# A group-normalised row LSTM: the second half's scale in two parts, and the work around the first row of the loop rearranged

## The chip, the cores and the metric

The kernel runs on one core of a Trainium2 chip. The time is the device time of one execution in microseconds; with several runs it is their median. The engines are TensorE (PE; its weight loads are PEld), VectorE (DVE), ScalarE (ACT), GpSimd (POOL) and SyncE (SP, which here only issues transfers). All arithmetic is in float32.

## The reference

The input x has shape (8, 96, 128, 128): images, channels, rows, columns. It is group-normalised (32 groups of three channels, statistics over a whole image), and then a row LSTM runs down the 128 rows, each row needing the state of the row above; the result is added to x.

```python
its = conv_1x3(_gn(x), W_is * mask) + b_is      # input taps: left and own column
def step(carry, row_in):                        # scan over the 128 rows
    h, c = carry
    ss = conv_3(h, W_ss) + b_ss                 # state taps: left, own, right column
    gates = ss + row_in                         # 4*96 channels
    f, i, o = sigmoid(...); g = tanh(...)       # four gates in three blocks of 32 channels
    c_new = f * c + i * g
    h_new = o * tanh(c_new)
    return (h_new, c_new), h_new
out = x + hs
```

## The kernel before

**Two halves and two stages.** The eight images are two halves of four (`NH` = 2, `BH` = 4). Stage one reads all of x once for the statistics of the group norm. Stage two is a loop of 256 half steps: half step n is row n // 2 of half n % 2. Two half steps are under way at a time, so that one half's gates are made while TensorE works on the other's products.

**The statistics.** An image goes through a ring of six buffers in six chunks of 2048 columns (`CH`), each of them four pieces of 512. VectorE takes the statistics of a chunk piece by piece (`bn_stats`, L676). Chunks 2 and 4 of all images but the last are ScalarE's (`sums_of`): it needs a column `base`, the negative of the chunk's first column, as a bias, which GpSimd makes (L207). It then sums the chunk and its squares (L208, L211). `merge` on GpSimd joins both engines' figures. A ring buffer is filled again when its reader is done.

**The scale.** `Scale` makes from the statistics the scale `rstd` and the shift `nmr` of a half: `means` and `squares` are small products on TensorE with the group matrix `gm`; `to_sbuf` copies their results from PSUM to SBUF for GpSimd; `scale` adds the epsilon, makes a first guess of the inverse root with two integer operations on VectorE (L275, L280), and refines it in three rounds.

**Work placed among the statistics.** The dictionary `events` holds what is issued after a certain statistics piece: `at(image, n)` is the n-th of 24 pieces of an image. Half 0 has its scale at images 4 (`at(4, 1)` to `at(4, 6)`), its first row's taps at images 4 and 5, and its first half step at images 5 and 6 (`begin` and the entries after it). Every engine works through its own instructions in the order in which they are issued.

**The row's operands.** `hx` holds the previous row's state in 96 partitions and, in the last 32, the normalised channels 64 to 96 of the row, which share the product with the state (`normalise_shared`, `shared_rows`). Of `hx` come three moving operands: the total `vs` and the difference `vf` on VectorE and the shifted differences `vd` on GpSimd, which is told to start after VectorE's (`shifted`). The other 64 channels' taps are `xs`, made by `widen` (normalise into even and odd columns, into `xw` or, for rows 1 to 3 of the first block of half 1, into a buffer of the ring called `late`) and `combine` on GpSimd (`own_image`, `own_row`).

**The half step.** TensorE's products are named by a figure or letter and a block: 1 with `vs`, 2 with `vf`, 0 and 3 with `vd`, P, Q and E with `xs`; the blocks A, B, C are 128 gate channels each, in one PSUM bank. `cp` copies a block's first half with the bias (ScalarE, or VectorE for block A), and `lo` and `hi` on VectorE make the even and odd columns of it, which 0 and 3 then add to. `ta` and `si` are tanh and sigmoid, `fg gt ce th ou` the cell, `S F D` the next row's total, difference and shifted difference, `re` the residual. `PERIOD` is the order of one half step in the loop; a part already done is skipped, and `'`, `+` and `*` stand for the half step before, the next and the one after that.

**The hand-over.** After the last statistic, half 1's scale is made (on VectorE), then its first row's shared channels, operands and own taps, then the taps of rows 1 to 3, then the products of half step 1 in the order of `do(1, ...)`, and the loop begins. `spin` issues products that nobody reads.

## Time and profile before

| What | Figure |
|---|---|
| Median of three runs | 2081.72 us (2080.5 to 2082.07) |
| The profiled execution | 2080.96 us |
| Its span, first to last instruction | 2079.2 us |
| Mean granted TensorE clock | 0.990 |
| Last statistic of VectorE ends | 136.47 us |
| First product of half step 1 starts | 144.83 us |
| First product of half step 2 (2A) starts | 160.19 us |
| PE busy from 160.19 us to the end | 1910.94 of 1919.01 us |

Times within the profile are counted from the first instruction. The device time is 1.76 us longer than the span. In the timeline a line is a group of equal instructions: start, time in us, engine, source line, operation, output and inputs, how many; in brackets the idle time before it and what ended it. In the chain of waits a line is a start, a time and what the end of the program waited for. In a table of windows each engine has its busy time and, in brackets, its instructions; behind them stand the granted clock of TensorE, the share of the transfer engines and GB/s.

### The profile page before, as it was taken

To read this page: it belongs to the slowest core of one execution; us is meant where nothing else is said; L and a number is where in the kernel's file an instruction comes from. 1 tells how busy PE (TensorE), PEld (TensorE's weight loads), DVE (VectorE), ACT (ScalarE), POOL (GpSimd) and SP (SyncE) were. 2 spreads that over 40 slices of the span, in tenths; PEclk is the share of its full clock that TensorE was granted. 3 is DMA by queue.
4 is the path that set the end of the run, shared out by engine and by line. 5 is a ranking of instruction groups with operands and counts; after the bars stand their busy time and mean duration, and the time that the engine had idled before them with its cause. 6 is when DMAs were issued, how large, how long until landed. Compare 5 with 4: busy or idle time off the path is not lost.

```text
span 2079.2 us, 31230 instructions
## 1 busy us (share of the span) xinstructions
PE 1950.6 (94%) x10810; PEld 1588.2 (76%) x10810; DVE 1684.7 (81%) x3494; ACT 1355.3 (65%) x2389; POOL 1435.0 (69%) x1615
## 2 busy tenths in 40 slices
PE   0249999999999999999999999999999999999998
PEld 0138888888888888888888888888888888888886
DVE  5677888888888888888888888888888888888887
ACT  4656666666666666666666666666666666666666
POOL 2326877777777777777777777777777777777762
PEclk9969999999999999999999999999999999999999
DMA  9991434443333444333334443333444333344411
GB/s 380 403 321 35 112 92 112 112 112 88 76 81 91 112 112 112 96 74 89 89 102 112 112 107 78 80 92 92 112 112 112 91 76 80 90 112 112 112 31 31
DMA packets 103325, 236.24 MB, mean 114 GB/s; under 512 B 5953, under 2 KB 8897, under 8 KB 97281
## 3 DMA queue, kind: packets, MB, share of 16 engines
q1 hardware_dynamic: 103168, 234.25, 41.2%
q8 instruction: 87, 1.43, 0.3%
q14 instruction: 70, 0.57, 0.1%
HBM read 183.90 MB, written 50.33 MB: 113 GB/s over the span
## 4 chain that ended last, share of the span: by engine, by line
PE 93%; DMA 3%; ACT 2%; POOL 1%; DVE 1%; issue 0%; SPq 0%; ACTq 0%; POOLq 0%; DVEq 0%
PE ps L384 92%; DMA piece<-in_x_dram 1%; DMA wt<-in_w_own_dram 1%; DMA xs<-in_x_dram 1%; ACT piece L208 0%; ACT piece L211 0%; ACT xs L208 0%; ACT xs L211 0%; DVE bst L676 0%; PE pv L246 0%; ACT g L436 0%; POOL xs L322 0%; POOL xs L321 0%; POOL xw L304 0%; ACT piece L302 0%
## 5 line engine op out<-in xcount | busy, mean ns | idle before, releaser
L384 PE MATMUL ps<-vd,wl 128*128 128x256 f32 x3072 | 815.7, 388 | 3.7 <-DVE ps L433 3.7
L436 ACT ACTIVATE g<-ps 32x512 f32<-32x512 f32 x768 | 453.6, 591 | 455.2 <-PE ps L384 446.8
L384 PEld LDWEIGHTS ps<-vd,wl 128*128 128x128 f32 x3072 | 562.5, 190 | 155.9 <-issue 86.5
L484 POOL TENSOR_TENSOR vd<-hx 128x512 f32<-128x512 f32 x256 | 265.9, 1039 | 483.9 <-DVE vs L474 480.5
L384 PE MATMUL ps<-xs,wx 64*128 64x256 f32 x3072 | 459.1, 395 | 14.9 <-POOL xs L321 14.9
L384 PE MATMUL ps<-vs,wm 128*128 128x256 f32 x1536 | 458.4, 380 | 0.0
L384 PE MATMUL ps<-vf,wm 128*128 128x256 f32 x1536 | 457.6, 380 | 0.0
L440 ACT ACTIVATE ps<-ps 96x512 f32<-96x512 f32 x768 | 418.6, 572 | 16.5 <-PE ps L384 0.2
L384 PEld LDWEIGHTS ps<-xs,wx 64*128 64x128 f32 x3072 | 323.6, 187 | 123.7 <-issue 84.9
L444 DVE TENSOR_TENSOR ps<-ps,c 96x512 f32<-96x512 f32 x256 | 178.0, 695 | 266.7 <-ACT ps L440 266.7
L433 DVE TENSOR_TENSOR ps<-m,ps 128x256 f32<-128x256 f32 x768 | 329.3, 429 | 26.3
L429 DVE TENSOR_TENSOR ps<-m,ps 128x256 f32<-128x256 f32 x768 | 324.9, 423 | 13.8 <-ACT m L426 5.0
L501 POOL TENSOR_TENSOR x<-x,hx 96x512 f32<-96x512 f32 x254 | 328.7, 1294 | 0.0
L384 PEld LDWEIGHTS ps<-vs,wm 128*128 128x128 f32 x1536 | 292.4, 191 | 40.6 <-DVE vf L479 0.7
L384 PEld LDWEIGHTS ps<-vf,wm 128*128 128x128 f32 x1536 | 292.5, 190 | 40.5 <-DVE vf L479 0.4
L426 ACT ACTIVATE m<-ps,wl 128x256 f32<-128x256 f32 x513 | 243.0, 474 | 74.0 <-PE ps L384 60.3
L322 POOL TENSOR_TENSOR xs<-xw 128x512 f32<-128x512 f32 x253 | 270.1, 1068 | 0.0
L384 PE MATMUL ps<-xs,wt 64*128 64x256 f32 x1536 | 265.3, 377 | 0.1
L454 ACT ACTIVATE th<-c 96x512 f32<-96x512 f32 x256 | 161.5, 631 | 105.5 <-DVE c L450 105.5
L304 POOL TENSOR_SCALAR hx<-x,rstd,nmr 32x512 f32<-32x512 f32 x248 | 199.9, 806 | 25.5
L384 PEld LDWEIGHTS ps<-xs,wt 64*128 64x128 f32 x1536 | 195.6, 188 | 18.6 <-issue 0.7
L304 POOL TENSOR_SCALAR xw<-xr,rstd,nmr 128x512 f32<-128x512 f32 x252 | 203.6, 808 | 0.8 <-DMA xr<-in_x_dram 0.4
(94 smaller groups left out, 1265.3 us busy)
## 6 DMA issues: line engine op xcount, KB each, us to landing
xr<-in_x_dram SPq DMA_DIRECT2D x124, 512.0 KB, 6.7
x<-in_x_dram SPq DMA_DIRECT2D x63, 768.0 KB, 5.8
out_dram<-x SPq DMA_DIRECT2D x62, 768.0 KB, 4.7
xs<-in_x_dram SPq DMA_DIRECT2D x30, 1024.0 KB, 11.9
piece<-in_x_dram SPq DMA_DIRECT2D x16, 1024.0 KB, 10.8
x<-in_x_dram SPq DMA_DIRECT2D x62, 256.0 KB, 3.1
xs<-in_x_dram SPq DMA_DIRECT2D x4, 512.0 KB, 7.8
out_dram<-x SPq DMA_DIRECT2D x2, 576.0 KB, 3.7
```

The costliest lines, as they stand in the source:

```text
L304: engine.tensor_scalar(dst, src, scale, shift, ALU.mult, ALU.add)
L322: nc.gpsimd.tensor_sub(differences, strided(xw[:, 0, :], 0, [(W + 1, n), (J, 2), (1, J)]), strided(xw[:, 0, :], J + 1, [(W + 1, n), (0, 2) ...
L384: nc.tensor.matmul(self.ps[a][:, bass.ts(half, HB)], weights[rows, bass.ts(a, P)], rhs[rows], start=new, stop=False, skip_group_check=True,)
L426: nc.scalar.activation(self.m1[a], m1, AF.Identity, bias=column)
L429: nc.vector.tensor_add(self.ps[a][:, 0:HB], self.m1[a], self.ps[a][:, HB:])
L433: nc.vector.tensor_sub(hi, self.m1[a], hi)
L436: nc.scalar.activation(self.g[a * 32 : (a + 1) * 32], self.ps[a][C:P], AF.Tanh)
L440: nc.scalar.activation(gate, gate, AF.Sigmoid)
L444: nc.vector.tensor_mul(f, f, self.c)
L454: nc.scalar.activation(self.th, self.c, AF.Tanh)
L484: diff = nc.gpsimd.tensor_sub(self.vd.rearrange("p t (b j) -> p t b j", b=BH), strided(h, 1, [(BH * JP - 1, 2), (JP, BH), (1, J)]), stride ...
L501: (nc.gpsimd if row + 1 < NT else nc.vector).tensor_add(xo, xo, self.h)
```

## The change

- The column `base` is made by ScalarE itself, with an activation of scale -1.
- `Scale` takes a range of images. Half 1 has two of them: the first three images' scale is made during the last image's statistics (`next_means`, `squares`, `to_sbuf`, `variance`, `guess`, at `at(7, 1)` to `at(7, 13)`), with GpSimd refining it, and only the last image's after them (`final`).
- `next_row`, at `at(7, 13)`, makes the first row of these three images: shared channels and widening on ScalarE; total, difference, shifted difference and own taps on GpSimd. What is left of the row after the last image is that image's.
- Half 0's variance moves from `at(4, 6)` to `at(4, 5)`, and its guess and scale to `at(4, 13)`.
- The memset of the buffer for rows 1 to 3 comes before the last image's scale. These rows' shared channels go from ScalarE, behind the own taps, to GpSimd, ahead of them.
- `do(1, ...)` has the own taps directly after blocks A and B's first products; 1C, 2C, the copies and the even and odd columns are left to `PERIOD`'s first round.

```diff
     def sums_of(b, i, xc):
         if i == 0:
-            nc.gpsimd.tensor_scalar(base[:, b : b + 1], xc[:, 0:1], -1.0, None, ALU.mult)
+            nc.scalar.activation(base[:, b : b + 1], xc[:, 0:1], AF.Identity, scale=-1.0)
...
     class Scale:
-        def __init__(self, s):
-            self.st, self.rstd, self.nmr = st[s], rstd[s], nmr[s]
+        def __init__(self, s, lo, hi):
+            n, self.name = hi - lo, f"{s}_{lo}"
+            self.st, self.rstd, self.nmr = (
+                st[s][:, lo:hi], rstd[s][:, :, lo:hi], nmr[s][:, :, lo:hi]
+            )
...
+        def variance(self, engine):
+            engine.tensor_scalar(self.v, self.pv, GN_EPS, None, ALU.add)
+
+        def guess(self):
...
+            nc.vector.tensor_scalar(
+                bits, self.v.bitcast(integer), 1, None, ALU.arith_shift_right
+            )
+            nc.vector.tensor_scalar(
+                self.rstd.bitcast(integer), bits, 0x5F3759DF, -1.0, ALU.subtract, ALU.mult
+            )
...
-        def total(self):
-            e, o = self.pair()
-            self.vs = self.tile("vs", (P, HB))
-            self.last = nc.vector.tensor_add(self.vs.rearrange("p (b j) -> p b j", b=BH), e, o)
+        def total(self, engine=nc.vector, lo=0, hi=BH):
+            e, o = self.pair(lo, hi)
+            self.last = engine.tensor_add(self.operand("vs")[:, 0, lo:hi], e, o)
...
+    def next_means():
+        merge(1, BH - 1)
+        late.append(Scale(1, 0, BH - 1))
+        late[0].means()
+
+    def next_row():
+        late[0].scale(nc.gpsimd)
+        shared_rows(nc.scalar, 1, 0, 1, range(BH - 1))
+        for j in range(BH - 1):
+            widen(nc.scalar, xw[1], j, 1, 1, j, 0)
+        step = half_step(1)
+        step.total(nc.gpsimd, 0, BH - 1)
+        step.difference(nc.gpsimd, 0, BH - 1)
+        step.shifted(0, BH - 1)
+        own_row(xw[1], 1, 0, 0, BH - 1)
...
-        at(4, 6): lambda: A.scale(nc.gpsimd),
+        at(4, 5): lambda: A.variance(nc.gpsimd),
+        at(4, 13): lambda: (A.guess(), A.scale(nc.gpsimd)),
...
-        at(7, 1): lambda: merge(1, BH - 1),
+        at(7, 1): next_means,
+        at(7, 4): lambda: (late[0].squares(nc.scalar), late[0].to_sbuf()),
+        at(7, 6): lambda: late[0].variance(nc.gpsimd),
+        at(7, 13): lambda: (late[0].guess(), next_row()),
...
-    Bh = Scale(1)
-    Bh.means()
-    Bh.squares(nc.vector)
+    rows = ring[2][:, 0 : (R - 1) * BH * (W + 1)].rearrange("p (r q) -> p r q", q=W + 1)
+    nc.gpsimd.memset(rows[:, :, J : J + 1], 0.0)
+    final = Scale(1, BH - 1, BH)
+    final.means()
+    final.squares(nc.vector)
     spin(5, wt[0][:, 0:256])
-    Bh.scale(nc.vector)
-
-    shared_rows(nc.vector, 1, 0, 1)
-    do(1 - NH, "S F")
+    final.variance(nc.vector)
+    final.guess()
+    final.scale(nc.vector)
+    shared_rows(nc.vector, 1, 0, 1, (BH - 1,))
+    step = half_step(1)
+    step.total(lo=BH - 1)
+    step.difference(lo=BH - 1)
+    widen(nc.scalar, xw[1], BH - 1, 1, 1, BH - 1, 0)
+    own_row(xw[1], 1, 0, BH - 1, BH)
+    step.shifted(BH - 1, BH)
+
     for j in range(BH):
-        widen(nc.scalar, xw[1], j, 1, 1, j, 0)
-    own_row(xw[1], 1, 0)
-    do(1 - NH, "D")
-    late = ring[2][:, 0 : (R - 1) * BH * (W + 1)].rearrange("p (r q) -> p r q", q=W + 1)
-    nc.gpsimd.memset(late[:, :, J : J + 1], 0.0)
-    for j in range(BH):
-        widen(nc.scalar, late, j, R - 1, 1, j, 1, step=BH)
+        widen(nc.scalar, rows, j, R - 1, 1, j, 1, step=BH)
+    shared_rows(nc.gpsimd, 1, 1, R)
     for r in range(1, R):
-        own_row(late[:, (r - 1) * BH : r * BH], 1, r)
-    shared_rows(nc.scalar, 1, 1, R)
+        own_row(rows[:, (r - 1) * BH : r * BH], 1, r)
...
-    do(1, "1A 2A 1B 2B 1C 2C PA PB QA QB P+A PC QC cpA loA hiA cpB loB hiB cpC loC hiC")
+    do(1, "2A 1A 2B 1B PA PB QA QB PC P+A QC")
```

## The prediction

> **What bounds the kernel now.** I read the page first (busy shares, then the shares of the chain), then the chain of waits in the gap between the two stages, then the timelines of single engines there, and last the one-microsecond windows with the granted clock. From the page:

> ```profile
> PE 1950.6 (94%) x10810; PEld 1588.2 (76%) x10810; DVE 1684.7 (81%) x3494; ACT 1355.3 (65%) x2389; POOL 1435.0 (69%) x1615
> PE 93%; DMA 3%; ACT 2%; POOL 1%; DVE 1%; issue 0%; SPq 0%; ACTq 0%; POOLq 0%; DVEq 0%
> ```

> TensorE (PE) carries the row loop. In the windows from 160.19 us to the end, PE is busy 1910.94 of 1919.01 us, and the change leaves the loop's order from the second half step on as it is. So it can only move what lies before 160.19: the statistics (VectorE's last one ends at 136.47) and the hand-over to the loop. The chain of waits in the hand-over:

> ```profile
> 146.14 1.03 POOL vd L484
> ...
> 147.28 0.74 ACT piece L302
> ...
> 150.33 0.74 ACT hx L302
> ...
> 153.35 0.48 ACT m L426
> ...
> 153.86 0.44 DVE ps L429
> ...
> 154.32 0.44 DVE ps L433
> ...
> 154.81 10.29 PE ps L384 x42
> ```

> GpSimd's shifted difference holds up the memset queued behind it (147.12); that holds ScalarE's four late widenings (`piece`, 3.03 us), then four shared rows (`hx`, 3.00 us), and only then comes the copy of block B (`m`), on which VectorE's even/odd pair and TensorE's product 0B wait. TensorE sees it so:

> ```profile
> 140.42 4.61 PE L171 MATMUL spin<-wl 128*128 128x256 f32 x10
> 144.83 1.06 PE L384 MATMUL ps<-vs,wm 128*128 128x256 f32 x2
> ...
> 148.06 2.00 PE L384 MATMUL ps<-xs,wx 64*128 64x256 f32 x14
> 150.78 1.10 PE L384 MATMUL ps<-vd,wl 128*128 128x256 f32 x4 [0.72 <-DVE ps L433]
> 154.81 1.22 PE L384 MATMUL ps<-vd,wl 128*128 128x256 f32 x2 [2.93 <-DVE ps L433]
> ...
> 160.19 0.59 PE L384 MATMUL ps<-vf,wm 128*128 128x256 f32 x2
> ```

> One product is two records. Two stalls, 0.72 and 2.93 us; at 160.19 the next half step begins. The windows (PEclk is the figure behind the engines) show a second loss:

> ```profile
> 151.00:152.00 1.00, 0.88 (x4) 0.43 (x3) 0.00 (x0) 0.93 (x3) 1.00 (x2) 1.00 1.02 246
> 152.00:153.00 1.00, 0.00 (x0) 0.00 (x0) 0.00 (x0) 0.97 (x2) 1.00 (x3) 0.88 1.08 227
> 153.00:154.00 1.00, 0.00 (x0) 0.00 (x0) 0.14 (x1) 0.97 (x3) 1.00 (x2) 0.50 1.10 223
> ...
> 159.00:160.00 1.00, 1.00 (x6) 0.34 (x5) 0.00 (x0) 0.24 (x1) 0.00 (x0) 0.71 0.46 100
> ```

> The clock falls in the long stall and stays at half until 159.x.

> **The change part by part: the load stage.**
> ScalarE's own column. Seven columns leave GpSimd. On ScalarE I take 0.2 us each, from its nearest rows (128x4 Square 0.17, 128x8 copy 0.18); bounds 0.1 and 0.35. It takes away waits of 11.55 us (image 1, behind the weights) and 5.05 us (image 4, behind the half-0 scale on GpSimd). But transfers bound most of this stage: their share is 1.0 in nearly every 4 us window to 136. The one hole is 88 to 92 (0.63, some 1.5 us), after image 4's late column kept a ring slot. It should close.
> That 1.5 us should not reach the end. From 103.44 to 134.7 VectorE is busy except for one wait of 0.83 us; it, not the transfers, is then the bound, and its start follows GpSimd's four own images. So I follow VectorE.
> Half 0's variance moves one slot up and its guess from (4,6) to (4,13). Today VectorE stands 3.59 us for it (to 80.63). In the new place the first piece of chunk 3, due at 80.4 by the 2.49 us pace of the chunks, ends at 81.06; the guess follows and GpSimd's scale starts at 81.6 instead of 81.16, less the 0.19 us column: own images +0.25 us. All of `begin` follows them: +0.25. Image 6's column stands in ScalarE's queue ahead of the cell tanh (116.48): +0.2. So VectorE starts image 7 0.45 us late, and the new guess (two operations, 0.2 us each) adds 0.4. Its wait for the last transfer (0.49) absorbs the rest: +0.36 at 136.47. Bounds: 0 to +1.0.
> At (7,1) to (7,13), three images' scale. The 14 merge operations end at about 125.2 (124.8 today); half 0's chain from merge to variance took 3.4 us (77.2 to 80.6), so 128.7. VectorE reaches (7,13) at about 129.85, so it does not wait; margin 1.1 us. GpSimd's 14 scale operations take 4 us (half 0: 81.16 to 85.09), to 134.3; six ScalarE pieces of 0.42 us beside it. GpSimd's total, difference, shifted difference and own row of three images, by its rows 128x256 0.64 and 128x512 1.06: 0.54 + 0.54 + 0.85 + 0.54 + 0.85 = 3.3 us, then the memset 0.12: done near 139.5. The final image's first GpSimd work comes at 143.3, so this costs nothing; uncovered it would cost 3 to 7 us. The three images' means stand in PE's queue ahead of the spin of ten, which only shifts. SyncE issues the same transfers in the same order.

> **The hand-over.** The final image's chain (aggregate, seven small products, 15 small VectorE operations at 0.2) is as long as today's: sizes 1 and 2 instead of 4 and 8 save nothing at 0.17 us each. Scale and shift ready: 142.40 + 0.36 = 142.8.
> VectorE then does one shared row (0.35) instead of four (1.51), and total and difference of 64 columns, 0.2 each; up to 0.4 beside GpSimd's own row, as today's difference took 0.87 beside GpSimd and 0.43 without. Ready by 144.0. But TensorE is in its spin of five until about 144.7: today the last weight load of the spin ended at 144.31 and the first product loaded at 144.59, so the lead is worth little. First product at 145.05 against 144.83: +0.2.
> GpSimd: own row of one image (0.33 + 0.43), shifted difference 0.43, to 144.7; four shared rows of 32x384, by the row 32x512 at 0.80 at most 0.8 each: 147.9; three own rows at 1.68: 152.9, against 155.26 today. First reader of those is the half step after next, near 158.
> ScalarE: one widening 0.42, then four at 0.74, 142.9 to 146.3. The four shared rows are off it. The copy of B is behind nothing then.
> TensorE: 2A 1A 2B 1B, own taps from 147.4 (today 144.83 to 147.1 for the same four), seven own products 2.0 to 149.4, 1C 2C 0.86, 0A 3A 0.86, 0B at 151.1. VectorE's side: copy of A 1.16 after the own taps start, as today (148.06 to 149.22), then copy, two even/odd pairs, 0.52 + 4 x 0.46, and 0.15 to the reader: 0B may start 3.67 us after the own taps start; TensorE arrives after 3.72. A tie; I take 0.2 us of waits, bounds 0 and 0.8.
> The sum: stalls 0.72 + 2.93; the stretch 154.81 to 160.19 (5.38 us) at full clock is 0B 0.43, eight own products 1.92 (as at 172.77 to 174.69), 3B 0.54 = 2.89, so 2.49 back. 6.14 - 0.2 (start) - 0.2 (waits) = **5.7 us**.
> The profiled execution's own 2080.96 would become 2075.3, its span 2073.5. The median shown, 2081.72, is 0.76 above the profiled one; I take the gain from it: **2076.0**.

> [...] The row shows the clock falling 1 us into the stall (0.88 in 152 to 153). I go with the row: 5.7. [...]

> **The rivals.**
> 1. The clock stays low in part: the stall goes, but short waits or a later rise keep half clock for the new stretch. [...] Against: today clock 1.00 from 146 to 152 across a 0.72 us wait. Gain 2.5 to 4: 2078.5. Chance 0.15.
> 2. More: the later spin leaves TensorE warm at the final image, the spin of five takes 2.2 us less, and the product starts when the difference lands (144.1), or the closed transfer hole shows at the end. Against: after the spin today the clock was down 3.5 us later. Gain 7 to 8.7: 2073.7. Chance 0.08.
> 3. It does not do what it says: another wait takes the copy's place (late rows on GpSimd holding its next work, or the own row of the final image), or the guess eats it. GpSimd's 5 us of slack speaks against. Gain 0 to 2: 2080.7. Chance 0.05.
> 4. Slower: the second guess stands in VectorE's stream at (7,13), with eleven statistics queued behind it and the last of them the bound. If the variance comes after 129.85, each microsecond of wait is one at the end. The point from which it decides is 5.7 us: variance after 135.6. The chain would have to take twice half 0's 7.0 us (73.56 to 80.6); at 137.8 the time is 2084.0. Half 0's guess did wait 3.59 us, but one slot after its copies. Chance 0.03, half of it past 0.2%.

> **How the numbers follow.** The main case has 0.69, gain 4.3 to 7.3. About 0.2% (4.2 us) is what a measurement of this kernel can tell from no change. Faster: main 0.68, rival 2 0.08, a little of rival 1: 0.78. Slower 0.02. Same 0.20. The range runs from 2073.2 to 2079.3: down to rival 2, up over rival 1; outside lie rivals 3 and 4 and the ends of the others.

> **What would show it.** Right: no stall over 0.5 us on PE between the spin of five and the loop, clock 1.00 from about 146.5 on, ScalarE's copy of B near 149, the loop's second half step at 154.5, VectorE's last statistic within 1 us of 136.8, no hole at 88 to 92. Wrong: a wait of VectorE for GpSimd's variance at (7,13); clock at 0.5 after 148; PE waiting for `xs` from GpSimd after 155; or a row loop longer than 1919 us.

## The result, and the profile after

| | before | after |
|---|---|---|
| Median of six runs each | 2081.48 us (2080.50 to 2082.07) | 2075.69 us (2074.33 to 2077.35) |
| Ratio of after to before | | 0.9973, 95% interval 0.9961 to 0.9986 |
| Profiled execution, its span | 2080.96, 2079.15 us | 2074.40, 2072.62 us |
| Last statistic ends | 136.47 us | 137.39 us |
| First product of half step 1 | 144.83 us | 145.11 us |
| 2A of the second half step | 160.19 us | 153.68 us |
| From there to the end | 1918.96 us | 1918.95 us |

The change makes the kernel 5.8 us faster. (The 1919.01 us given for before counts to the rounded span of 2079.2.) The three stretches say where the 6.5 us between the two spans lie: last statistic +0.92, hand-over (last statistic to 2A) 23.72 to 16.29, which is -7.43, and row loop -0.01. The page of the kernel after, busy shares and shares of the chain:

```profile
PE 1950.5 (94%) x10824; PEld 1589.7 (77%) x10824; DVE 1683.4 (81%) x3493; ACT 1356.9 (65%) x2398; POOL 1441.1 (70%) x1632
PE 93%; DMA 3%; DVE 2%; ACT 1%; POOL 1%; issue 0%; SPq 0%; POOLq 0%
```

The shares hardly move: the work is the same, and a gain of 0.3% in one stretch doesn't show here. The chain of waits in the hand-over, kernel after:

```profile
137.41 0.82 DVE st L721
...
140.63 0.85 PE dm L252 x4
141.48 3.79 PE spin L171 x10
145.27 19.76 PE ps L398 x110
```

Before, the chain ran through GpSimd's `vd`, ScalarE's `piece`, `hx` and `m` and VectorE's `ps` pair. Now it goes from the statistics through the small products and the spin into TensorE's products and stays there. TensorE's timeline, kernel after:

```profile
141.34 3.93 PE L171 MATMUL spin<-wl 128*128 128x256 f32 x10
145.11 0.59 PE L398 MATMUL ps<-vf,wm 128*128 128x256 f32 x2
...
146.93 2.00 PE L398 MATMUL ps<-xs,wx 64*128 64x256 f32 x14
148.86 0.70 PE L398 MATMUL ps<-vs,wm 128*128 128x256 f32 x2
...
149.82 1.46 PE L398 MATMUL ps<-vd,wl 128*128 128x256 f32 x6
151.21 1.34 PE L398 MATMUL ps<-xs,wx 64*128 64x256 f32 x9
...
153.14 0.70 PE L398 MATMUL ps<-vd,wl 128*128 128x256 f32 x2
153.68 0.59 PE L398 MATMUL ps<-vf,wm 128*128 128x256 f32 x2
```

No line has brackets: there is no wait between the spin and the loop. The six records at 149.82 are 0A, 3A and 0B in one piece. The windows of the kernel after, with the granted clock behind the five engines:

```profile
144.00:145.00 1.00, 1.00 (x5) 0.82 (x4) 0.21 (x2) 0.03 (x1) 0.00 (x0) 0.78 1.12 243
...
152.00:153.00 1.00, 1.00 (x12) 0.74 (x8) 0.00 (x0) 0.00 (x0) 1.00 (x2) 1.00 1.06 248
153.00:154.00 1.00, 1.00 (x6) 0.78 (x5) 0.00 (x0) 0.73 (x2) 1.00 (x3) 1.00 1.06 238
```

The clock rises within the spin (0.78 in 144 to 145) and is 1.00 in 152 to 154, where it fell before.

### The profile page after: what moved, and what is told of

The parts are those of the page before. It is cut to its first block, busy times and chain, and to the rows that moved or that the text cites. A ratio compares the mean times of both kernels' runs of the same rounds, so it can differ in the third digit from the quotient of the medians.

```text
span 2072.6 us, 31273 instructions
## 1 busy us (share of the span) xinstructions
PE 1950.5 (94%) x10824; PEld 1589.7 (77%) x10824; DVE 1683.4 (81%) x3493; ACT 1356.9 (65%) x2398; POOL 1441.1 (70%) x1632
## 4 chain that ended last, share of the span: by engine, by line
PE 93%; DMA 3%; DVE 2%; ACT 1%; POOL 1%; issue 0%; SPq 0%; POOLq 0%
PE ps L398 93%; DMA piece<-in_x_dram 3%; DVE bst L715 1%; PE spin L171 0%; ACT g L450 0%; POOL xw L313 0%; POOL xs L331 0%; POOL xs L330 0%; ACT ps L454 0%; ACT piece L208 0%; ACT piece L211 0%; ACT xs L211 0%; ACT xs L208 0%; PE pv L252 0%; SPq L704 0%
## 5 line engine op out<-in xcount | busy, mean ns | idle before, releaser
L331 POOL TENSOR_TENSOR xs<-xw 128x512 f32<-128x512 f32 (+1 forms) x254 | 270.4, 1065 | 0.0
L313 POOL TENSOR_SCALAR hx<-x,rstd,nmr 32x512 f32<-32x512 f32 (+1 forms) x252 | 202.7, 805 | 26.0
```

What stands on the lines that cost most here:

```text
L313: engine.tensor_scalar(dst, src, scale, shift, ALU.mult, ALU.add)
L331: nc.gpsimd.tensor_sub(differences, strided(xw[:, 0, :], 0, [(W + 1, n), (J, 2), (1, J)]), strided(xw[:, 0, :], J + 1, [(W + 1, n), (0, 2) ...
```

## The experiments

The theory: the gain is the second stall and the clock that it costs; both go because ScalarE's copy of block B no longer stands behind GpSimd's shifted difference (through the memset) and the shared rows. Rivals: the split scale earns it by an earlier first product; TensorE's new order earns it by itself; the load stage does, through ScalarE's own column. All experiments in one table first. "Hand-over" is measured in each profile from the end of the last statistic to 2A (where the order starts otherwise, to the first product of the second half step); from there to the end it is 1918.7 to 1919.7 us in every kernel.

| Kernel | stat ends | to first product | from it to 2A | hand-over | median, us | ratio to before (95%) |
|---|---|---|---|---|---|---|
| before | 136.47 | 8.36 | 15.36 | 23.72 | 2081.48 | |
| after | 137.39 | 7.72 | 8.57 | 16.29 | 2075.69 | 0.9973 (0.9961 to 0.9986) |
| e1_order_only | 138.73 | 8.93 | 8.65 | 17.58 | 2076.94 | 0.9973 (0.9962 to 0.9984) |
| e2_split_only | 136.46 | 8.36 | 12.38 | 20.74 | 2080.91 | 0.9993 (0.9984 to 1.0002) |
| e3_act_rows | 136.28 | 8.36 | 10.12 | 18.48 | 2077.90 | 0.9978 (0.9969 to 0.9987) |
| e4_before_filled | 137.78 | 8.16 | 13.31 | 21.47 | 2079.74 | 0.9987 (0.9978 to 0.9995) |
| e5_after_again | 139.98 | 7.72 | 8.57 | 16.29 | 2075.92 | 0.9968 (0.9956 to 0.9981) |
| e6_loads_ahead | 139.30 | 7.88 | 8.57 | 16.45 | 2076.49 | one run |
| e7_warm | 137.10 | 7.17 | 8.64 | 15.81 | 2074.01 | 0.9962 (0.9949 to 0.9976) |
| e8_split_again | 136.53 | 8.35 | 14.83 | 23.18 | 2081.22 | one run |
| e9_memset_first | 136.61 | 8.16 | 10.10 | 18.26 | 2075.95 | 0.9973 (0.9963 to 0.9983) |
| e10_product_order | 136.51 | 8.93 | 15.27 | 24.20 | 2082.48 | 0.9999 (0.9990 to 1.0009) |
| e11_pool_column | 138.36 | 7.85 | 8.57 | 16.42 | 2075.72 | 0.9967 (0.9955 to 0.9979) |
| e12_no_spin | 138.16 | 6.97 | 11.53 | 18.50 | 2076.93 | 0.9975 (0.9965 to 0.9984) |

The first column needs care. Kernels with the same load stage end their statistics up to 3.7 us apart (136.28 in e3, 139.98 in e5). Of this, 2.8 us is there when half 0's first product begins (94.78 and 97.61), behind the stretch that waits for transfers; most of the rest comes with the clock, which rises 6.75 us after that product in e3 and 8.47 us after it in e5, and half pace (in e3 0.85 us a product ahead of the rise, 0.43 behind it) for 1.72 us more costs 0.86. One profile's span therefore says little; the hand-over, counted from the last statistic, repeats (16.29 twice for the kernel after).

**e1: the new order without the split.** The kernel before, with the memset early, the late shared rows on GpSimd ahead of the own rows, and the new `do(1, ...)`.

```diff
+    nc.gpsimd.memset(late[:, :, J : J + 1], 0.0)
     Bh = Scale(1)
...
-    nc.gpsimd.memset(late[:, :, J : J + 1], 0.0)
     for j in range(BH):
         widen(nc.scalar, late, j, R - 1, 1, j, 1, step=BH)
+    shared_rows(nc.gpsimd, 1, 1, R)
...
-    shared_rows(nc.scalar, 1, 1, R)
...
-    do(1, "1A 2A 1B 2B 1C 2C PA PB QA QB P+A PC QC cpA loA hiA cpB loB hiB cpC loC hiC")
+    do(1, "2A 1A 2B 1B PA PB QA QB PC P+A QC")
```

> The kernel before with only the order of the hand-over changed: memset first, late shared rows on GpSimd ahead of the own rows, the new order of the first products; no scale in two parts, no column on ScalarE. Theory (the gain is ScalarE's queue ahead of block B's copy, and the clock that fell in the stall): nearly all of it, no PE stall over 0.5 us after the spin of five, second half step at 154.5, 5 to 6 us faster than before, 2075.5 to 2076.5. Rival (the gain is the three images made ahead, so that less is left after the last one): at most 1.5 us, 2080 or more.

Measured: hand-over 17.58, -6.14; median 5.5 us under before's 2082.41 on that chip. Its first product waits for VectorE's difference of all four images; its second half step comes in the kernel after's time, 8.65 later. TensorE's timeline of e1:

```profile
147.66 0.67 PE L384 MATMUL ps<-vf,wm 128*128 128x256 f32 x2 [0.70 <-DVE vf L479]
...
156.31 0.59 PE L384 MATMUL ps<-vf,wm 128*128 128x256 f32 x2
```

So the split is not what earns the gain. It is worth 1.29 us more in the hand-over (17.58 to 16.29); in the medians this can't be told from nothing.

**e2 and e8: the split without the new order.** Both are the same program: the kernel after with the memset, the shared rows and `do(1, ...)` as before.

```diff
-    nc.gpsimd.memset(rows[:, :, J : J + 1], 0.0)
     final = Scale(1, BH - 1, BH)
...
     step.shifted(BH - 1, BH)
+    nc.gpsimd.memset(rows[:, :, J : J + 1], 0.0)
...
-    shared_rows(nc.gpsimd, 1, 1, R)
     for r in range(1, R):
         own_row(rows[:, (r - 1) * BH : r * BH], 1, r)
+    shared_rows(nc.scalar, 1, 1, R)
...
-    do(1, "2A 1A 2B 1B PA PB QA QB PC P+A QC")
+    do(1, "1A 2A 1B 2B 1C 2C PA PB QA QB P+A PC QC cpA loA hiA cpB loB hiB cpC loC hiC")
```

> The changed kernel with the hand-over's order as before: memset behind the shifted difference, late shared rows on ScalarE behind the own rows, the old order of the first products; scale in two parts and column on ScalarE stay. Theory: ScalarE's copy of block B waits behind the memset, four widenings and four shared rows until 153, the stall of 2.5 to 3 us and the fall of the clock are back; within 1 us of before, 2080.5 to 2082. Rival: 4 us or more faster than before, 2077.5 or less.

> The kernel with the old order of the hand-over again, for a second profile: its times fall into 2077 to 2078 and 2080.5 to 2082, and in the profile taken, of the first sort, the clock stayed at 1.00 through a stall of 2.29 us. [...]

Measured: e2 is not told from before (interval 0.9984 to 1.0002), although two of its eleven runs stand at 2077.0 and 2078.0, the others between 2079.3 and 2082.0. The stall is back in both profiles, and they show one way in which the runs can differ. TensorE's timeline of e2, then its window around the stall:

```profile
154.10 0.70 PE L398 MATMUL ps<-vd,wl 128*128 128x256 f32 x2 [2.29 <-DVE ps L447]
...
157.20 0.59 PE L398 MATMUL ps<-vf,wm 128*128 128x256 f32 x2
```
```profile
153.00:154.00 1.00, 0.00 (x0) 0.00 (x0) 0.81 (x3) 0.49 (x2) 1.00 (x2) 1.00 1.07 238
```

and the same two views of e8:

```profile
153.82 1.22 PE L398 MATMUL ps<-vd,wl 128*128 128x256 f32 x2 [1.80 <-DVE ps L447]
...
159.71 0.64 PE L398 MATMUL ps<-vf,wm 128*128 128x256 f32 x2
```
```profile
152.00:153.00 1.00, 0.02 (x1) 0.00 (x0) 0.12 (x1) 0.97 (x3) 1.00 (x2) 0.98 1.05 217
153.00:154.00 1.00, 0.17 (x1) 0.18 (x2) 0.97 (x3) 0.21 (x1) 1.00 (x2) 0.50 1.06 242
```

The longer stall (2.29) keeps the clock, the shorter (1.80) loses it. From 0B to the next half step it is 3.10 us in e2 and 5.89 in e8. So the length of the stall alone does not decide; the last section says where each of the two lay.

**e9: the memset alone.** One instruction of the kernel before is moved.

```diff
+    nc.gpsimd.memset(late[:, :, J : J + 1], 0.0)
     Bh = Scale(1)
...
     do(1 - NH, "D")
-    nc.gpsimd.memset(late[:, :, J : J + 1], 0.0)
```

> The kernel before with one thing changed: the memset of the late rows' buffer comes before the last image's scale, so that ScalarE's four late widenings no longer stand behind GpSimd's shifted difference (3.11 us). Theory: the copy of block B ends near 150.8 instead of 153.8, TensorE's second stall of 2.93 us all but goes and the clock stays up; the first, 0.72 us, stays: 5 us or so faster than before, some 2077.5, though the shared rows are still on ScalarE. Rival (it takes GpSimd's taking over the shared rows): 0 to 2 us faster.

Measured: 2075.95 against 2082.00 on the same chip, 0.9973: all of the gain that the medians can tell. In the profiles the hand-over is 5.46 us shorter, in the kernel after 7.43. ScalarE's timeline of e9:

```profile
144.22 3.03 ACT L302 ACTIVATE piece<-xr,nmr,rstd 128x384 f32<-128x384 f32 x4
147.27 3.03 ACT L302 ACTIVATE hx<-x,nmr,rstd 32x384 f32<-32x384 f32 x4
150.32 0.84 ACT L426 ACTIVATE m<-ps,wl 128x256 f32<-128x256 f32 x2
```

and TensorE's:

```profile
150.54 1.94 PE L384 MATMUL ps<-vd,wl 128*128 128x256 f32 x6 [0.73 <-DVE ps L433]
...
154.87 0.59 PE L384 MATMUL ps<-vf,wm 128*128 128x256 f32 x2
```

The shared rows still stand ahead of the copy of B, but everything on ScalarE begins as soon as the scale is there, and the copy comes at 150.32 instead of 153.35. The wait of 0.73 stays; the long one is gone, and with it the fall of the clock. Taking the shared rows away from ScalarE and reordering the products were not needed for this.

**e10: the products' order alone.** The last hunk of e1 by itself.

> The kernel before with only the new order of the first products. Theory: the 0.72 us stall goes, since 1C and 2C stand between the copy of block A and 0A, but 0B waits as long as before for block B's copy at 153.8, so that the other stall grows by as much; within 1 us of before. Rival (the order of the products brings the gain): 3 us or more faster.

Measured: 2082.48, no change. TensorE's timeline of e10:

```profile
154.88 1.22 PE L384 MATMUL ps<-vd,wl 128*128 128x256 f32 x2 [3.62 <-DVE ps L433]
```

The short stall is gone, the long one has grown from 2.93 to 3.62: product 0B starts at 154.88 against 154.81. TensorE only waits elsewhere for the same copy.

**e3: the late shared rows on ScalarE again**, in the kernel after.

```diff
-    shared_rows(nc.gpsimd, 1, 1, R)
     for r in range(1, R):
         own_row(rows[:, (r - 1) * BH : r * BH], 1, r)
+    shared_rows(nc.scalar, 1, 1, R)
```

> The changed kernel with one thing undone: the late rows' shared channels are on ScalarE again, behind the widenings. Theory: the copy of block B ends near 152.0 and 0B waits some 2.3 us; with the clock kept, 2.3 us slower than the changed kernel (2078.0), with the clock falling up to 4.8 us slower (2080.5). Rival: the same as the changed kernel.

Measured: hand-over 18.48, +2.19; median 2077.90, some 2 us above the kernel after, with intervals that overlap. TensorE's timeline of e3 has one wait again:

```profile
151.67 0.70 PE L398 MATMUL ps<-vd,wl 128*128 128x256 f32 x2 [0.65 <-DVE ps L447]
```

The rows themselves cost this 0.65; a wait of some 2.3 had been expected, but ScalarE's copy of B came at 150.21 and was done before 152.0. Of the rest, 0.64 is the later first product and 0.63 the first four products, in part at half clock: here the clock rose only after the spin (first product 1.06 us, in the kernel after 0.59).

**e4: the clock by itself.** The kernel before, with six unread products (twelve records) in the stall ahead of 0B.

```diff
     do(1, "1A 2A 1B 2B 1C 2C PA PB QA QB P+A PC QC cpA loA hiA cpB loB hiB cpC loC hiC")
+    do(1, "0A 3A")
+    spin(6, wt[0][:, 0:256])
```

> The kernel before with six products that nobody reads put between 3A and 0B, where TensorE stands 2.93 us; they take 2.6 us at full clock, so the stall itself stays as long. Theory (the idle time makes the clock fall, and the cold stretch behind it costs 2.49 us): clock 1.00 from 152 to 160, second half step near 157.7, 2079.0. [...]

Measured: 2079.74, 2.7 us less than before on that chip. TensorE's timeline of e4:

```profile
152.65 2.75 PE L171 MATMUL spin<-wl 128*128 128x256 f32 x12
156.15 0.70 PE L384 MATMUL ps<-vd,wl 128*128 128x256 f32 x2 [0.75 <-DVE ps L433]
...
159.25 0.59 PE L384 MATMUL ps<-vf,wm 128*128 128x256 f32 x2
```

TensorE waits for the same copy as long as before, but stays busy, and the clock is 1.00 in every window from 152 to 155. From 0B to the next half step it takes 3.10 us instead of 5.38. This 2.28 us is the clock's part of the loss.

**e5 and e6: the kernel after again, and its late loads ahead.** e5 is unchanged. e6 loads rows 1 to 3 image by image.

```diff
-    load_rows(1, 0, 1, R)
-    load(1, 0, 1, R)
+    for j in range(BH):
+        for p in range(2):
+            nc.sync.dma_start(
+                xr[1][p * C2 : (p + 1) * C2, j, W : R * W],
...
+    for j in range(BH):
+        for c0, c1, p0 in ((C2, C, C), (0, C, 0)):
+            nc.sync.dma_start(
+                xt[1, 0][p0 : p0 + c1 - c0, j, 1:R, :].rearrange("c r w -> c (r w)"),
...
```

> The changed kernel once more, for a second profile and on the same chip as the next. If the spread of its times (2074.33 to 2077.35) comes from the point at which the clock rises and from the transfers of the statistics, both differ again from the first profile, and what lies between the last statistic and the second half step stays within 1.5 us of 16.3 us. Time 2075 to 2077.

> The changed kernel with the late rows of half 1 loaded image by image, which leaves their order but takes away SyncE's wait for ScalarE's shared rows (12.8 us, to 136.5). Theory (the spin of five, not the transfers, sets the first product): the transfers go out from 124 on, no hole from 131 to 137, ScalarE's last widening starts near 143 instead of 145, the first product and the time stay, 2074 to 2077. Rival (the late transfers cost time): 1.5 us or more from the last statistic to the second half step.

They test what the profile after showed and the prediction had not foreseen. SyncE's waits, kernel after:

```profile
SPq L155 <- ACT hx L311: 12.8, 1, 12.8
```

SyncE's timeline:

```profile
122.44 1.29 SPq L704 DMA_DIRECT2D xs<-in_x_dram  x3
136.53 0.33 SPq L155 DMA_DIRECT2D x<-in_x_dram  x1
```

ScalarE's timeline:

```profile
144.97 0.50 ACT L311 ACTIVATE xw<-xr,nmr,rstd 128x128 f32<-128x128 f32 x1 [7.15 <-DMA xr<-in_x_dram]
```

and the window of 132 to 136 us, with the transfers' share last but one:

```profile
132.00:136.00 4.00, 1.31 (x7) 1.07 (x6) 4.00 (x8) 0.99 (x2) 2.11 (x11) 0.50 0.00 0
```

The load of rows 1 to 3 waits 12.8 us for ScalarE's shared row of the first three images, the transfers idle, and the last image's widening waits for a transfer until 144.97. In e6 that widening waits for the scale (VectorE's `nmr`), as the prediction had it. Yet e6's hand-over is 16.45 and its time 2076.49: the late load cost nothing, because TensorE's own taps begin at 146.93 and GpSimd's own row, at 145.55, was in time.

**e7: TensorE warm at the last image.** e6, with `gt ce th` in one place and the second guess four pieces later, and 16 unread products instead of ten.

```diff
-        at(6, 9): lambda: do(0, "gt"),
-        at(6, 12): lambda: do(0, "ce th"),
+        at(6, 8): lambda: do(0, "gt ce th"),
...
-        at(7, 13): lambda: (late[0].guess(), next_row()),
-        at(7, 20): lambda: spin(10, stats[6]),
+        at(7, 17): lambda: (late[0].guess(), next_row()),
+        at(7, 20): lambda: spin(16, stats[6]),
```

> The kernel of the run before with three steps more: half 0's gt, ce and th together ahead of ScalarE's sums of image 6 (VectorE waited 1.51 us for th), the three images' guess at the 17th piece instead of the 13th, and sixteen instead of ten unread products before the last image's means, so that the clock is up for them. Theory: last statistic some 1.3 us earlier, the spin of five 2.2 us instead of 3.9 to 4.6 and the first product as soon as the difference lands, 0.9 us more: 2073 to 2074 beside 2075.7. Rival (the clock falls again, or the spin holds up the means): no gain, or up to 1 us slower.

Measured: 2074.01, 1.9 us under e5 on the same chip, with intervals that overlap. It is the lowest median of the study, but not told from the kernel after. Its hand-over is 15.81, 0.48 less. The clock was up for the last image's means, but it fell again at 139.48 and rose at 142.90, so the spin of five took 3.79 us and not the 2.2 expected. No run takes the steps one by one. TensorE's timeline of e7:

```profile
144.27 0.67 PE L398 MATMUL ps<-vf,wm 128*128 128x256 f32 x2 [0.40 <-DVE vf L496]
```

The first product now waits for VectorE's difference, so more of this kind would bring nothing there.

**e11: the column on GpSimd again**, in the kernel after.

```diff
-            nc.scalar.activation(base[:, b : b + 1], xc[:, 0:1], AF.Identity, scale=-1.0)
+            nc.gpsimd.tensor_scalar(base[:, b : b + 1], xc[:, 0:1], -1.0, None, ALU.mult)
```

> The changed kernel with the column on GpSimd again. In GpSimd's queue image 4's column now stands ahead of half 0's scale, whose guess came to a later place, so the hole of the transfers at 88 to 92 stays closed, and image 1's wait behind the weights costs nothing while transfers bound. Theory: within 1 us of the changed kernel, 2075 to 2077. Rival (the column is worth its place): 1.5 us or more slower.

Measured: 2075.72, no loss. The window 88 to 92 us, kernel before:

```profile
88.00:92.00 4.00, 0.00 (x0) 0.00 (x0) 4.00 (x8) 3.97 (x5) 3.73 (x5) 1.00 0.63 203
```

kernel after:

```profile
88.00:92.00 4.00, 0.00 (x0) 0.00 (x0) 4.00 (x8) 3.80 (x6) 3.62 (x6) 1.00 1.01 422
```

and e11:

```profile
88.00:92.00 4.00, 0.00 (x0) 0.00 (x0) 3.97 (x8) 3.88 (x6) 3.70 (x6) 1.00 1.02 426
```

The transfers' hole is closed without ScalarE's column, so the column did not close it; the rest of the new load stage, which e11 keeps, did. (The share is 0.41 to 0.63 in all five profiles with the old load stage, 1.00 to 1.02 in all nine with the new one.) No run isolates which part. Nor does the load stage earn the gain: e1 and e9 have the old one, hole included.

**e12: without the spin of five**, in the kernel after.

```diff
-    spin(5, wt[0][:, 0:256])
```

> The changed kernel without the five unread products ahead of the first row's. Theory (clock): the first product starts some 0.8 us earlier, when the difference lands, but the clock comes up only 3 to 5 us into the products, which run at half speed until then: 1 to 2.5 us slower than the changed kernel. Rival (the spin only holds TensorE up): 0.8 us faster.

Measured: 2076.93 against 2075.72 for e11 on the same chip, 1.2 more, with intervals that overlap; hand-over 18.50, +2.21. TensorE's timeline of e12:

```profile
145.13 1.19 PE L398 MATMUL ps<-vf,wm 128*128 128x256 f32 x2 [2.88 <-DVE vf L496]
...
148.81 3.09 PE L398 MATMUL ps<-xs,wx 64*128 64x256 f32 x14
```

The first product comes 0.75 sooner after the statistics, when its operand lands, but the products run at half clock until 151.07, and the second half step comes 2.96 later after it. In the profiles the spin is worth more than it delays; the medians don't settle it.

## Why the prediction was right

**The cause.** Right: the stall and the clock. e4 measures the clock's part at 2.28 us (predicted 2.49), e9 shows that the stall goes with the head of its chain, the memset behind GpSimd's shifted difference. The prediction put this gain down to three edits together, the memset, the shared rows and the products' order. By the medians the first is enough. ScalarE's copy of B came at 148.32 (predicted near 149), and the clock was 1.00 from 144.44 on (predicted 146.5).

**The hand-over's sum.** 2A came at 153.68, predicted 154.5. The terms that were mis-sized: the first four products took 1.82 us and not 2.27, because the clock rose inside the spin; the tie at 0A and 0B cost nothing instead of 0.2; and the record of the two products ahead of the stall was 0.23 longer (1.10 before, with the stall behind it; 0.87 of the run now), so the stall was worth that much more. The prediction's path had this in it (151.1 + 0.2 + 2.89 is 154.2), its sum did not. First product 145.11 (predicted 145.05) is right by two errors that cancel: the statistics ended 0.56 later than forecast, the spin was 0.68 shorter. Luck has a part in the total too: the two profiled executions lie 6.56 us apart, and that the medians, from runs up to 3 us apart, differ by 5.79 where 5.7 was predicted does not make every term right.

**The load stage.** Last statistic +0.92 in these two profiles, predicted +0.36, inside the bounds. Own images +0.20 (predicted 0.25), image 6's column +0.24 (predicted 0.2) and the two operations of the guess +0.27 (predicted 0.4) are right. Not in the sum: the point at which the clock rises in half 0's first products. They ran at half pace, 0.85 us each, up to the first entry in the trace's record of the granted clock, a rise, at 101.55 before and 103.48 after; the windows' figure of 1.00 ahead of it only means that there is no record yet. The rise came 6.71 us after the first of these products (94.84) before and 8.44 us after it (95.04) in the kernel after, and half pace for 1.73 us more costs 0.86. Together with the first two terms this is the 1.30 by which the cell tanh was late (`th` at 117.78, before 116.48), and VectorE started image 7 1.25 us late instead of 0.45. The late rise is not the change's doing: it came 8.7 and 8.8 us after in e4 and e1, with the old load stage, and 6.2 to 6.8 in e2, e3 and e8, with the new one. With a scatter of 3.7 us between profiles, the +0.92 is no property of the change. That the closed hole would not reach the end held: transfers were done near 131, VectorE at 137.4. But the prediction put the hole down to the late column, and e11 closes it with the column back on GpSimd.

**The second guess (rival 4).** GpSimd's line for the three images' variance and VectorE's for the guess, both in the kernel after's timeline of these engines:

```profile
129.26 0.25 POOL L276 TENSOR_SCALAR v<-sums 128x6 f32<-128x6 f32 x1 [3.14 <-ACT sums L272]
...
130.49 0.15 DVE L282 TENSOR_SCALAR t<-v 128x6 int32<-128x6 int32 x1
```

The variance was ready 1.0 us ahead (predicted margin 1.1), and GpSimd had the three images and the memset done at 139.8 (predicted 139.5).

**What it missed.** "SyncE issues the same transfers in the same order" is true of the order and wrong as a cost of nothing: the load behind the new reader went out at 136.53 instead of near 122, with 5 us of transfers idle. It was covered, as e6 shows, but the prediction had not named the cover.

**The clock's fall (rival 1).** The prediction took the fall from its row, 1 us into the stall, and that held: stalls of 2.93 (before), 1.80 (e8) and 3.62 us (e10) each lost the clock, 0.9 to 2.6 us in. Rival 1 did not come. Its gain of 2.5 to 4 us was the author's estimate; the changed kernel shows no half clock behind the first product, in neither of its profiles: the clock rose ahead of it (144.44 against 145.11 in the first, 147.04 against 147.70 in e5) and stayed at 1.00 into the loop.

## What to carry to other kernels

Follow a chain of waits back to its head before rebuilding the middle: here three engines' work was rearranged, and one memset of 0.12 us, queued behind an instruction that it did not need, held up most of it. Count a stall of TensorE at its length plus, where the clock falls in it, what half clock behind it costs (2.28 us here, e4), and if it can't be removed, fill it with unread products (2.7 us in e4's median). When a new reader of a buffer is put early, look at what the transfer queue has next for that buffer.

## What the runs showed of the hardware

**When it falls.** Counted from the rise, the fall in the hand-over came after 6.83 us (before, 145.93 to 152.75), 6.83 (e8, 146.14 to 152.97) and 10.24 (e10, 143.59 to 153.83): two, two and three times the 3.41. In the 3.41 us up to the fall TensorE was idle for only 1.59, 1.67 and 2.57 us, and for 1.55 up to e7's fall at 139.48. e2's longer stall lay across one of the points (152.63), with 1.54 us of idle time in the 3.41 us before it (an earlier wait of 0.73 counted in) and 1.48 in those behind it, and kept the clock. So e8's shorter stall had more idle time on one side of a point than e2's longer one, which a point split. 1.54 and 1.55 us are too close to name a threshold, and no run varied the idle time by itself.

**When it rises.** From the start of the spin to full clock it took 3.1 us in the kernel after (to 144.44) and 5.5 in the one before (to 145.93), from 2.8 (e7) to 5.7 (e3) over all profiles; without a spin, from the first product, 5.9 (e12). The same spin of five thus takes 3.93 or 4.61 us, as the rise comes earlier (144.44, after) or later (145.93, before). That, and the 3.7 us of scatter in the load stage, is why single profiles of this kernel can't settle a microsecond, and why the medians of e1, e3, e5, e9 and e12, though their hand-overs differ by up to 2.2 us, are not told apart.
